# Turning normalised h of layers 0 and 1 by transposing DMA on 16-bit planes instead of by TensorE

## The chip, the cores and the metric

The kernel runs on one core of a Trainium2 chip. The metric is the device time of one execution in microseconds (us), and the time of a kernel is the median of its runs. Before the change it is 1192.94 us (three runs, 1192.58 to 1193.06).

## The reference, cut to what matters

Four graph layers work on x of shape (8, 2048, 64), float32, with one adjacency matrix adj of 2048 x 2048. Each layer normalises x, takes the positive part and adds what the layer makes of it:

```
h = max(layernorm(x), 0)                     # before every layer
# layer 0: w = einsum(embedding, weight), per node; b = embedding @ bias
x = x + sum_k einsum(A_k h, w[:, k]) + b     # A_0 = I, A_1 = adj, A_2 = 2 adj adj - I
# layer 1: v = h with node 0 replaced by intervention_value, then 3 times:
v = relu([v, adj v] @ W1.T + b1) @ W2.T + b2
x = x + v
# layer 2: x + ((adj h / sqrt2) mixed by w_nl, + b_nl) @ w_out.T + b_out
# layer 3: x + elu(softmax over neighbours with adj > 0.5, or over all nodes) applied to h
```

What matters here is that layers 0 and 1 need h in two positions. The products with adj want the nodes on the partitions. The term A_0 h of layer 0 and the first v of layer 1 want the features on the partitions, so that a small weight matrix can be applied to them. A block of h is therefore turned: 128 x 512 numbers with nodes on the partitions become 128 x 512 numbers with features on the partitions.

## The kernel before, in words

The 8 samples go in 4 pairs p (two samples of 64 features fill 128 columns), and the 2048 nodes in 4 blocks nb of 512. A block is a tile of 128 partitions x 4 x 128 float32, 256 KB. The matrix lies in SBUF as BT with entries 0 or 1. A product of h with it (`chunks`, L261) takes 16 chunks of 128 nodes, and in each two matmuls, one with the high part H of h and one with the rest L; the result is scaled by a row `crow` on VectorE (`scaled`, L246).

**Layer 0.** A prologue (up to about 84 us) loads the matrix, normalises the pairs 0 and 1, writes their h to the DRAM tensors hs and makes their first products. Then, for each p and nb (loop at L805 to L881), TensorE makes the second product t2T (32 matmuls) and then, in `node_weights` (L767), for each of four t twelve pairs of matmuls y (L781) of the turned terms t0T, t1T, t2T with the weights. VectorE multiplies each y by the node's embedding and adds it up (L790, 16 times for each t), and y has two buffers. After the block `keep` (L759) normalises the result for layer 1, and stores h in hs and x in xs. In pass p = 0 every block also normalises a block of pair 2 (`norm_0(2, nb)`, L881); pair 3 is normalised in the products of pass p = 2.

A normalisation (`norm_stages`, L180) runs in three stages that later calls of `go_on` release: means and squares (ScalarE, tile sq, which has one buffer), variances (VectorE) and a power (GpSimd, L200), and the scaling of z (VectorE, L203, tile z with three buffers), after which `done` or `store` is called.

**The turning.** `to_feat` (L278) turns a block: four TensorE transposes into PSUM (`transposed`, L271, L275) and one ScalarE copy (L280). It serves two users. `feat_0` (L800) loads h of the next block (queue of ScalarE, tile hb_f) and turns it into t0T, between the product t2T of a block and its y matmuls. `begin_next` (L727) loads h of a pair of layer 1 (tile hb), overwrites the first node with the intervention value (L740) and turns it into gT. For pair 0 of layer 1 this happens in the last block of layer 0: `between` calls `first_operand(t)` (L743) after each t, which turns block t and multiplies it by a weight (`back_whole`, L715, the tile bn_u). For the pairs 1 to 3, `step1` (L942) calls it at chunks 4 and 12 of the last product of the pair before (dictionary `fill`, L1022) and at chunk 4 of its own first product (L997); `halve_two` (L748) then makes the operand from two blocks.

**Layer 1** makes three steps for each pair, each with four products of 32 matmuls, and small ones (ph L953, bn L708) between them. In the steps 0 and 1 VectorE also tests whether the matrix is what this path assumes (`test`, L911): `test_load` (L900) loads a strip of adj and a transposed strip mt of a copy of BT, by a transposing DMA of 128 x 512 two-byte numbers on the queue of SyncE (L908).

What sets the order: the program order above, from which the framework's scheduler makes one fixed order of instructions for each engine and queue when the kernel is built; `issue_after`, which puts one instruction behind another on its engine; and the `fill` dictionaries. At run time each engine and each queue takes its instructions in that order and waits where an operand or a buffer isn't ready.

Of the kernel before, what the change touches and what calls it, by code (L numbers as in the profile page):

```python
# [8 lines left out]
F32 = mybir.dt.float32  # L9
F32R = mybir.dt.float32r  # L10
BF16 = mybir.dt.bfloat16
I32 = mybir.dt.int32
U8 = mybir.dt.uint8
AF = mybir.ActivationFunctionType
ALU = mybir.AluOpType
AX = mybir.AxisListType
# [26 lines left out]
def uniform_path(  # L43
# [53 lines left out]
    biasD = dram.tile([P, NCH, C], F32, name="biasD")  # L97
    t1D = dram.tile([P, N], F32, name="t1D")
    MD = dram.tile([N, N], BF16, name="MD")

    def bank(tag, name):
        return psums[-1].tile([P, 512], F32, tag=tag, name=name)
# [51 lines left out]
    def load_h(p, nb, name, pool):  # L154
        t = pool.tile([P, 4, 2 * C], F32, tag="hb", name=f"hb_{name}", bufs=2 if lastp else 3)
        (nc.sync if lastp else nc.scalar).dma_start(t, hs[p][:, part(nb), :])
        return t

    def load_crow(nb, name, tag="crow"):
        t = work.tile([P, 512], F32, tag=tag, name=f"crow_{name}", bufs=2)  # L160
# [132 lines left out]
    def norm_0(p, nb, also=None, xt=None):  # L293

        def done(z):
            if also is not None:
                also(z)
            stored.append(
                (nc.gpsimd if xt is None else nc.scalar).dma_start(hs[p][:, part(nb), :], z)
            )  # L300

        if xt is not None:
            return norm_stages(xt, f"0_{p}_{nb}", done, None)
        norm_relu(load_x(0, p, nb), f"0_{p}_{nb}", done)
# [338 lines left out]
    def make_weights():  # L643

        col(b1[:, None], 1, "b1c", b1c)
        b2c = col(b2[:, None], 1, "b2c")
        bnl = col(b_nl[:, None], 1, "bnl")
        wn = col(w_nl, 2, "wnl")
        ws = consts.tile([P, 1], F32, name="wsum")

        raw = block("z", "wz0", 3)
        nc.gpsimd.memset(raw, 0.0)
        for i, w in enumerate((w1[:, :C], w1[:, C:], w2, w_out)):
            for hf in range(2):
                hs_ = slice(hf * C, (hf + 1) * C)
                nc.sync.dma_start(raw[hs_, i, hs_], w)
        yield
        tr, pr = (block("z", f"wz{i}", 3) for i in (1, 2))
        nc.vector.tensor_copy(tr, transposed(lambda t: raw[:, t, :], "wT"))
        nc.vector.tensor_copy(w1e, tr[:, 1])  # L660
        ps = psums[-1].tile([P, 4, P], F32, tag="tr", name="wP")
        b2b, bnb = b2c.to_broadcast([P, P]), bnl.to_broadcast([P, P])
        pairs = ((raw[:, 2], tr[:, 0]), (raw[:, 2], tr[:, 1]), (b2b, tr[:, 1]), (bnb, tr[:, 3]))
        for i, (lhsT, rhs) in enumerate(pairs):
            nc.tensor.matmul(ps[:, i, :], lhsT, rhs, start=True, stop=True)
        nc.vector.tensor_copy(pr, ps)
        p1 = bank("tr", "wb1s")
        nc.tensor.matmul(p1[:, :1], tr[:, 0], b2c, start=True, stop=True)
        nc.vector.tensor_tensor(b1s, p1[:, :1], b1c, op=ALU.add)

        fill_row(raw[:, 0, :], b_out)
        nc.vector.tensor_tensor(pr[:, 3, :], pr[:, 3, :], raw[:, 0, :], op=ALU.add)
        with tc.issue_after(chain[-1].ins):
            nc.vector.tensor_scalar(wn, wn, INV_SQRT2, None, op0=ALU.mult)
            nc.vector.tensor_tensor(ws, wn[:, 0:1], wn[:, 1:2], op=ALU.add)
        nc.vector.tensor_scalar(tr[:, 3, :], tr[:, 3, :], ws, None, op0=ALU.mult)
        for hf in range(2):
            with tc.issue_after(wt_load.ins):
                nc.sync.dma_start(ivt[:, hf * C:(hf + 1) * C], iv)
        nc.gpsimd.dma_start(wD[:, 0:4], tr)  # L680
        nc.gpsimd.dma_start(wD[:, 4:8], pr)
        yield


    w1e = consts.tile([P, P], F32, name="w1e")
    ivt = consts.tile([1, P], F32, name="ivt")

    def feat(i, name):

# [37 lines left out]
    def begin_next(n, q):  # L727

        if n >= len(items):
            return  # L730
        layer, p = items[n]
        nm = f"{layer}_{p}_{q}"
        hl, gT = ops.setdefault(n, ([], []))
        h = load_h(p, q, nm, lastp[0] if n else l0q)
        if layer == 2:
            hl.append(halves(h, nm))
            return
        if q == 0:
            with tc.issue_after(relus[-1].ins) if relus else nullcontext():
                nc.scalar.copy(h[0:1, 0, :], ivt)  # L740
        gT.append(to_feat(h, feat(0, f"gT_{nm}"), nm))

    def first_operand(q):  # L743
        begin_next(0, q)
        hl, gT = ops[0]
        hl.append(halves(back_whole(gT[q], w1e, f"u_{q}"), f"u_{q}"))

# [8 lines left out]
    def rows4(r, times=4):  # L756
        return r.rearrange("p (b c) -> p b c", b=2)[:, None].to_broadcast([P, times, 2, C])

    def keep(p, nb, acc, name, more):  # L759

        norm_relu(acc, name, lambda z: nc.gpsimd.dma_start(hs[p][:, part(nb), :], z))
        nc.gpsimd.tensor_tensor(nodes(acc), nodes(acc), more, op=ALU.add)  # L762
        kept.append(nc.gpsimd.dma_start(xs[p][:, part(nb), :], acc))

# [2 lines left out]
    def node_weights(p, nb, terms, between):  # L767
        acc = load_x(0, p, nb)
        bn = l0q.tile([P, 4, C], F32, name="bn", bufs=2)
        nc.sync.dma_start(bn, biasD[:, part(nb), :])  # L770

        odd = l0q.tile([P, 4, 2 * C], F32, name="odd")
        av, ov = nodes(acc), nodes(odd)
        for t in range(4):
            ts = slice(t * P, (t + 1) * P)
            for dg in range(D // DG):
                y = psums[-1].tile([P, 2, 512], F32, tag="big", name=f"y_{p}_{nb}_{t}_{dg}")
                for k in range(K):
                    for bb in range(2):
                        hs_ = slice(bb * C, (bb + 1) * C)  # L780
                        nc.tensor.matmul(  # L781
                            y[:, bb, :], terms[k][hs_, ts], wt[hs_, k, dg * 512:(dg + 1) * 512],
                            start=(k == 0), stop=(k == K - 1),
                        )
                for d in range(DG):
                    e = dg * DG + d
                    yd, ec = y[:, :, d * C:(d + 1) * C], emb[:, 4 * nb + t, e:e + 1]
                    xj = (av, ov)[d % 2][:, t]
                    old = xj if e != 1 else bn[:, t, None, :].to_broadcast([P, 2, C])
                    last = nc.vector.scalar_tensor_tensor(  # L790
                        xj, yd, ec, old, op0=ALU.mult, op1=ALU.add
                    )
            ahead.append(last)
            chain.append(last)
            go_on()
            between(nb, t)
        nc.vector.tensor_tensor(acc, acc, odd, op=ALU.add)
        keep(p, nb, acc, f"1_{p}_{nb}", b2r[:, None, None].to_broadcast([P, 4, 2, C]))

    def feat_0(p, q):  # L800
        h = h_first if p + q == 0 else load_h(p, q, f"f0_{p}_{q}", l0q)
        return to_feat(h, term(0, f"t0T_{p}_{q}"), f"0_{p}_{q}")

    first_t0 = []
    for p in range(NP):  # L805
        hl_next, t1T_next = [], []

# [18 lines left out]

        def between(nb, t):

            if 4 * p + nb + 1 == 4 * NP:
                first_operand(t)  # L830
            elif nb == 2 and t == 1:
                halve_next(0)
            elif nb == 3:
                halve_next(t + 1)
                if t == 0:
                    load_next(3)
# [16 lines left out]
        for nb in range(NB):  # L853
# [1 line left out]
            crow = load_crow(nb, nm)  # L855
            t2T = product(
                hl1, nb, nm, term(2, f"t2T_{nm}"), crow,
                fill={12: lambda: first_t0.append(feat_0(0, 0))} if p + nb == 0 else {},
                tag="mm" if p + nb else "b6",
            )  # L860
            if p + nb == 0:
                t0T = first_t0[0]
            go_on()
            t0T_next = feat_0(*divmod(4 * p + nb + 1, 4)) if 4 * p + nb + 1 < 4 * NP else None
            if p + nb == 0:
                pro.close()
                psums.append(ctx.enter_context(
                    tc.tile_pool(name="psum", bufs=2, space=bass.MemoryType.PSUM)
                ))
            if nb == 3:  # L870
                load_next(2)
            node_weights(p, nb, (t0T, t1T[nb], t2T), between)
            t0T = t0T_next
            if nb in (1, 2):
                load_next(nb - 1)
            with tc.issue_after(kept[-1].ins):
# [65 lines left out]
    def step1(n, p, st, hl, gT):  # L942
# [51 lines left out]
        halves_of = range(NCH // 2), range(NCH // 2, NCH)  # L994
        ps0 = sums_of(0)
        other = n > 0 and st == 0
        chunks(ps0, hl, 0, halves_of[0], {4: lambda: begin_next(n, 3)} if other else {})  # L997
        if carry:
            carry.pop()()
        if other:  # L1000
# [10 lines left out]
        add(1)  # L1011
        go_on()
        ps2 = sums_of(2)
        chunks(ps2, hl, 2, range(NCH))
        scale(ps2, 2)
        map_two(2)
        finish_two(0)
        add(2)
        go_on()
        fill = {}  # L1020
        if last:
            fill = {  # L1022
                4: lambda: (begin_next(n + 1, 0), begin_next(n + 1, 1)),
                9: lambda: halve_two(n + 1, 0), 12: lambda: begin_next(n + 1, 2),
            }
        ps3 = sums_of(3)
        chunks(ps3, hl, 3, range(NCH), fill)
# [740 lines left out]
```

## Time and profile before

| | |
|---|---|
| median of the runs | 1192.94 us |
| profiled execution, its own time | 1195.87 us |
| span of its profile | 1194.1 us |
| TensorE matmul (PE) busy | 1171.6 us, 98% |
| weight load (PEld) busy | 815.9 us, 68% |
| VectorE (DVE) busy | 744.7 us, 62% |
| ScalarE (ACT) busy | 235.5 us, 20% |
| GpSimd (POOL) busy | 230.8 us, 19% |
| transposes of L275 that turn h (hb_f, hb, h_first) | 60, 64 and 4 |
| transposing DMAs (mt, L908) | 64 |
| granted TensorE clock | 0.997 |

The profile comes from one execution, so its span is compared with its own time of 1195.87 us, 2.93 us above the median of the runs. In a group line the columns are line, engine, operation, output and inputs by the program's names, shapes and count. In a line of the timeline they are start in us, duration in us, engine, line, operation, and in brackets how long the engine was idle before it and what released it. Matmuls are pipelined: the distance between two starts is what one costs, and the duration shown is longer. "SPq", "ACTq" and "POOL ... DMA" are transfers being issued by a queue.

### The profile page before, as it was taken

What the parts mean: (1) busy time and instruction counts of PE and PEld (TensorE: products, weight loads), DVE (VectorE), ACT (ScalarE), POOL (GpSimd) and SP (SyncE); (2) the same over time, 40 slices, a digit from 0 to 9 for tenths busy, and PEclk for the clock granted to TensorE, in tenths of its full rate; (3) what the DMA queues carried; (4) which work ended last, traced back from release to release, by engine and by line L of the source; (5) the groups of instructions that cost most, each with busy time, mean ns of one, the idle gap of its engine ahead of it and who ended that gap; (6) DMA issues with size and microseconds to landing.
All of it is one profiled execution on the core that took longest, in us unless ns stands there. A gap on an engine that the chain in (4) does not pass through costs nothing.

```text
span 1194.1 us, 19514 instructions
## 1 busy us (share of the span) xinstructions
PE 1171.6 (98%) x7738; PEld 815.9 (68%) x7738; DVE 744.7 (62%) x1933; ACT 235.5 (20%) x372; POOL 230.8 (19%) x244
## 2 busy tenths in 40 slices
PE   8999999999999999999999999999999999999995
PEld 7775555555585555855547777777778777778884
DVE  5457888877847777267764446554644655465674
ACT  5620001000010000000012224333322433211110
POOL 5520221211121111001102004101300410241121
PEclk9999999999999999999999999999999999999998
DMA  9982334222241233212217634662763374351432
GB/s 359 330 209 66 93 102 119 84 67 79 81 141 45 75 82 100 78 31 73 69 55 195 132 80 129 173 142 72 193 132 83 125 177 103 106 170 60 136 114 74
DMA packets 99848, 141.24 MB, mean 118 GB/s; under 512 B 43772, under 2 KB 56572, under 8 KB 97700
## 3 DMA queue, kind: packets, MB, share of 16 engines
q1 hardware_dynamic: 81332, 79.43, 25.6%
q0 software_dynamic: 12256, 49.73, 13.9%
q10 hardware_dynamic: 6160, 10.75, 2.9%
q8 instruction: 63, 1.03, 0.3%
q14 instruction: 37, 0.30, 0.1%
HBM read 95.03 MB, written 35.66 MB: 109 GB/s over the span
## 4 chain that ended last, share of the span: by engine, by line
PE 90%; DVE 3%; DMA 3%; ACT 1%; POOL 1%; issue 1%; POOLq 0%; DVEq 0%; ACTq 0%
PE bv L264 38%; PE y L781 27%; DMA BT<-in_adj_dram 3%; PE bv_3b L264 3%; PE bv_2b L264 3%; PE bv_1b L264 3%; PE bv_0b L264 2%; PE bn L708 2%; PE ph L953 2%; PE pt L275 1%; PE bv_0a L264 1%; PE bv_3a L264 1%; PE bv_2a L264 1%; PE bv_1a L264 1%; DVE acc L790 1%
## 5 line engine op out<-in xcount | busy, mean ns | idle before, releaser
L264 PE MATMUL bv<-BT,H 128*128 128x512 f32 x768 | 303.4, 395 | 0.0
L264 PE MATMUL bv<-BT,L 128*128 128x512 f32 x768 | 299.3, 390 | 0.0
L790 DVE SCALAR_TENSOR_TENSOR acc<-y,emb,acc 128x128 f32<-128x128 f32 x512 | 176.2, 344 | 66.0 <-PE y L781 66.0
L264 PEld LDWEIGHTS bv<-BT,H 128*128 128x128 f32 x768 | 144.1, 188 | 37.1 <-PE bn L708 6.5
L264 PEld LDWEIGHTS bv<-BT,L 128*128 128x128 f32 x768 | 144.2, 188 | 29.0
L790 DVE SCALAR_TENSOR_TENSOR odd<-y,emb,odd 128x128 f32<-128x128 f32 x448 | 153.3, 342 | 0.0
L781 PE MATMUL y<-wt,t0T 64*128 64x512 f32 x512 | 143.7, 607 | 2.4 <-DVE odd L790 1.7
L200 POOL TENSOR_TENSOR rstd<-var,mhalf 128x8 f32<-128x8 f32 x64 | 106.5, 1665 | 169.5 <-DVE var L197 165.2
L192 ACT ACTIVATE sq<-z 128x512 f32<-128x512 f32 x64 | 40.4, 632 | 410.9 <-DVE z L187 382.7
L264 PE MATMUL bv<-BT,H_u 128*128 128x512 f32 x256 | 100.9, 394 | 0.0
L249 DVE TENSOR_TENSOR g<-bv,crow 128x512 f32<-128x512 f32 x48 | 33.2, 691 | 108.4 <-PE bv L264 107.9
L264 PE MATMUL bv<-BT,L_u 128*128 128x512 f32 x256 | 99.8, 390 | 0.0
L781 PEld LDWEIGHTS y<-wt,t0T 64*128 64x128 f32 x512 | 45.8, 185 | 63.2 <-issue 57.1
L762 POOL TENSOR_TENSOR acc<-acc,b2r 128x512 f32<-128x512 f32 x16 | 21.2, 1325 | 314.5 <-DVE z L187 314.5
L762 POOL TENSOR_TENSOR acc<-acc,wl 128x512 f32<-128x512 f32 x16 | 22.1, 1381 | 306.0 <-DVE z L187 305.4
L203 DVE SCALAR_TENSOR_TENSOR z<-z,rstd 128x512 f32<-128x512 f32 x64 | 43.6, 686 | 39.1 <-POOL rstd L200 39.1
L781 PE MATMUL y<-wt,t1T 64*128 64x512 f32 x256 | 66.8, 589 | 0.0
L264 PEld LDWEIGHTS bv<-BT,H_u 128*128 128x128 f32 x256 | 48.1, 188 | 13.2 <-issue 3.2
L187 DVE SCALAR_TENSOR_TENSOR z<-mean,acc 128x256 f32<-128x256 f32 x112 | 52.7, 514 | 5.2 <-DMA hs<-z 4.7
L264 PEld LDWEIGHTS bv<-BT,L_u 128*128 128x128 f32 x256 | 48.1, 188 | 9.7
L959 ACT COPY g<-ph 64x512 f32<-64x512 f32 x64 | 37.2, 582 | 77.8 <-PE ph L953 76.6
L916 DVE SCALAR_TENSOR_TENSOR junk<-mt,cols,st 128x512 uint8<-128x512 bf16 x64 | 47.9, 748 | 5.2 <-DMA mt<-MD 3.8
(228 smaller groups left out, 1743.4 us busy)
## 6 DMA issues: line engine op xcount, KB each, us to landing
BT<-in_adj_dram POOLq DMA_DIRECT2D x16, 1024.0 KB, 10.8
crow<-crowD SPq DMA_DIRECT2D x64, 256.0 KB, 3.5
st<-in_adj_dram SPq DMA_DIRECT2D x64, 256.0 KB, 4.0
hs<-z POOLq DMA_DIRECT2D x40, 256.0 KB, 3.2
xs<-acc POOLq DMA_DIRECT2D x32, 256.0 KB, 2.8
MD<-BT POOLq DMA_DIRECT2D x16, 512.0 KB, 5.3
acc<-xs SPq DMA_DIRECT2D x32, 256.0 KB, 4.6
hb<-hs SPq DMA_DIRECT2D x28, 256.0 KB, 3.3
```

The costliest lines, as they stand in the source:

```text
L187: firsts.append(nc.vector.scalar_tensor_tensor(split(z)[:, :, e], each(mean)[:, :, e, None].to_broadcast([P, 4, C]), -1.0 / C, nodes(xt)[: ...
L192: squares.append(nc.scalar.activation(sq, z, AF.Square))
L200: powers.append(nc.gpsimd.tensor_tensor(rstd, var, mhalf, op=ALU.pow))
L203: scales.append(nc.vector.scalar_tensor_tensor(groups(h), g, 0.0, rstd[:, :, None].to_broadcast([P, 8, C]), op0=ALU.max, op1=ALU.mult))
L249: ahead.append(nc.vector.tensor_tensor(to, ps.rearrange("p (q t) -> p t q", t=4), crow, op=ALU.mult))
L264: nc.tensor.matmul(ps, hl[m // 4][i][:, m % 4, :], BT[:, m, nb * 512:(nb + 1) * 512], start=(m == 0 and i == 0), stop=(m == NCH - 1 and i ...
L708: nc.tensor.matmul(ps[two[hf], bb, (4 * i + t) * C:(4 * i + t + 1) * C], fT[two[bb], at:at + C], wmat[two[bb], two[bb]], start=True, stop= ...
L762: nc.gpsimd.tensor_tensor(nodes(acc), nodes(acc), more, op=ALU.add)
L781: nc.tensor.matmul(y[:, bb, :], terms[k][hs_, ts], wt[hs_, k, dg * 512:(dg + 1) * 512], start=(k == 0), stop=(k == K - 1),)
L790: last = nc.vector.scalar_tensor_tensor(xj, yd, ec, old, op0=ALU.mult, op1=ALU.add)
L916: nc.vector.scalar_tensor_tensor(junk, mt, cols[:, i, :], st, op0=ALU.mult, op1=ALU.not_equal, accum_out=bad[:, i, q:q + 1],)
L959: nc.scalar.copy(gT[nb + i][two[bb], :], ph[bb][two[bb ^ i], :])
```

## The change

Turned h of both layers, but for the very first block, no longer comes from TensorE. Each block of normalised h is seen as 16-bit numbers and split on ScalarE into two planes, the low and the high halves (`store_planes`, two copies that read every second 16-bit number; they land in the tile sq). GpSimd's queue writes both planes to a DRAM tensor hp. SyncE's queue brings each plane back with a transposing DMA into a tile hb (`load_planes`, two DMAs), and ScalarE joins them (`join_planes`, two copies that write every second 16-bit number).

Blocks of layer 0 that the prologue has normalised are in hs only, so pass p = 0 loads seven of them again and splits them (`restage`, two in each block). The pairs 2 and 3 are split where they are normalised, and `keep` of layer 0 splits instead of storing h in hs. The calls of `begin_next` move: for pair 0 into the blocks 2 and 3 of the last pass, for the others partly from the last product of a pair to the one before it; `first_operand(3)` moves from the last block of layer 0 to chunk 7 of layer 1's first product. The intervention value becomes a column that is copied into gT after the join.

```diff
+    hp = [[
+        dram.tile([NB, 2, P, 512], U16, name=f"hp{layer}_{p}") for p in range(NP)
+    ] for layer in range(2)]
...
+    def bits(t):
+        return t.bitcast(U16)
+
+    def store_planes(h, layer, p, nb):
+
+        pl = bits(block("sq", f"pl_{layer}_{p}_{nb}", 1).rearrange("p t f -> p (t f)"))
+        hv = bits(h.rearrange("p t f -> p (t f)")).rearrange("p (q s) -> p s q", s=2)
+        pl = pl.rearrange("p (s q) -> p s q", s=2)
+        for s in range(2):
+            nc.scalar.copy(pl[:, s], hv[:, s])
+        nc.gpsimd.dma_start(hp[layer][p][nb].rearrange("s p q -> p s q"), pl)
+
+    def load_planes(layer, p, nb, pool):
+        t = pool.tile([P, 512], F32, tag="hb", name=f"pt_{layer}_{p}_{nb}", bufs=2 if lastp else 3)
+        pt = bits(t).rearrange("f (s n) -> f s n", s=2)
+        for s in range(2):
+            nc.sync.dma_start(
+                pt[:, s],
+                hp[layer][p][nb, s].rearrange("p (t f) -> (p t) f", t=4),
+                transpose=True,
+            )
+        return pt
+
+    def join_planes(pt, out):
+        ov = bits(out).rearrange("f (t n s) -> f s t n", t=4, s=2)
+        for s in range(2):
+            nc.scalar.copy(ov[:, s], pt[:, s].rearrange("f (n t) -> f t n", t=4))
+        return out
...
             stored.append(
                 (nc.gpsimd if xt is None else nc.scalar).dma_start(hs[p][:, part(nb), :], z)
             )
+            if xt is None:
+                store_planes(z, 0, p, nb)
...
-        for hf in range(2):
-            with tc.issue_after(wt_load.ins):
-                nc.sync.dma_start(ivt[:, hf * C:(hf + 1) * C], iv)
+        col(iv.rearrange("o c -> c o"), 1, "ivt", ivt)
...
-        h = load_h(p, q, nm, lastp[0] if n else l0q)
         if layer == 2:
-            hl.append(halves(h, nm))
+            hl.append(halves(load_h(p, q, nm, lastp[0]), nm))
             return
+        pt = load_planes(1, p, q, lastp[0] if n else l0q)
+        with tc.issue_after(relus[-1].ins) if relus else nullcontext():
+            gT.append(join_planes(pt, feat(0, f"gT_{nm}")))
         if q == 0:
-            with tc.issue_after(relus[-1].ins) if relus else nullcontext():
-                nc.scalar.copy(h[0:1, 0, :], ivt)
-        gT.append(to_feat(h, feat(0, f"gT_{nm}"), nm))
+            nc.scalar.copy(gT[0][:, 0:1], ivt)
 
     def first_operand(q):
-        begin_next(0, q)
...
+             lambda z, p, nb: store_planes(z, 1, p, nb))
...
+    def restage(times):
+
+        for _ in range(times):
+            p, q = divmod(len(restaged) + 1, NB)
+            if p > 1:
+                return
+            h = block("z", f"h_{p}_{q}", 3)
+            restaged.append(nc.sync.dma_start(h, hs[p][:, part(q), :]))
+            store_planes(h, 0, p, q)
...
+            if t == 2 and ahead_t0:
+                join_planes(*ahead_t0)
+            if p + 1 == NP and t == 3 and nb > 1:
+                begin_next(0, 3 * (nb - 2))
             if 4 * p + nb + 1 == 4 * NP:
-                first_operand(t)
+                if t == 0:
+                    begin_next(0, 2)
+                if t < 3:
+                    first_operand(t)
...
-            t0T_next = feat_0(*divmod(4 * p + nb + 1, 4)) if 4 * p + nb + 1 < 4 * NP else None
...
+            if p == 0:
+                restage(2)
             if nb == 3:
                 load_next(2)
+            if 4 * p + nb + 1 < 4 * NP:
+                at = divmod(4 * p + nb + 1, NB)
+                ahead_t0 = [load_planes(0, *at, l0q), term(0, "t0T_%d_%d" % at)]
+            if 4 * p + nb + 1 == 4 * NP:
+                begin_next(0, 1)
             node_weights(p, nb, (t0T, t1T[nb], t2T), between)
...
-        chunks(ps0, hl, 0, halves_of[0], {4: lambda: begin_next(n, 3)} if other else {})
+        fill = {}
+        if st == 0:
+            fill = {4: lambda: begin_next(n, 3)} if n else {7: lambda: first_operand(3)}
+        chunks(ps0, hl, 0, halves_of[0], fill)
...
-        chunks(ps2, hl, 2, range(NCH))
+        fill = {}
+        if last and n + 1 < NP:
+            fill = {5: lambda: begin_next(n + 1, 0), 11: lambda: begin_next(n + 1, 1)}
+        chunks(ps2, hl, 2, range(NCH), fill)
...
-        if last:
+        if last and n + 1 < NP:
+            fill = {6: lambda: begin_next(n + 1, 2), 9: lambda: halve_two(n + 1, 0)}
+        elif last:
             fill = {
                 4: lambda: (begin_next(n + 1, 0), begin_next(n + 1, 1)),
-                9: lambda: halve_two(n + 1, 0), 12: lambda: begin_next(n + 1, 2),
+                12: lambda: begin_next(n + 1, 2),
             }
```

More of the change, by code (lines that the diff above doesn't have):

```diff
@@ L13 @@
 U8 = mybir.dt.uint8
+U16 = mybir.dt.uint16
 AF = mybir.ActivationFunctionType
@@ L685, in uniform_path @@
     w1e = consts.tile([P, P], F32, name="w1e")
-    ivt = consts.tile([1, P], F32, name="ivt")
+    ivt = consts.tile([P, 1], F32, name="ivt")
     def feat(i, name):
@@ L757, in rows4, with store_h, keep @@
         return r.rearrange("p (b c) -> p b c", b=2)[:, None].to_broadcast([P, times, 2, C])
-    def keep(p, nb, acc, name, more):
-        norm_relu(acc, name, lambda z: nc.gpsimd.dma_start(hs[p][:, part(nb), :], z))
+    def store_h(z, p, nb):
+        nc.gpsimd.dma_start(hs[p][:, part(nb), :], z)
+    def keep(p, nb, acc, name, more, store=store_h):
+        norm_relu(acc, name, lambda z: store(z, p, nb))
         nc.gpsimd.tensor_tensor(nodes(acc), nodes(acc), more, op=ALU.add)
@@ L797, in node_weights @@
         nc.vector.tensor_tensor(acc, acc, odd, op=ALU.add)
[L798 to L804, printed above, removed]
+        keep(p, nb, acc, f"1_{p}_{nb}", b2r[:, None, None].to_broadcast([P, 4, 2, C]),
+             lambda z, p, nb: store_planes(z, 1, p, nb))
+    first_t0, restaged = [], []
+    def restage(times):
[6 more added lines that the diff above has]
+            store_planes(h, 0, p, q)
     for p in range(NP):
@@ L857, in uniform_path @@
                 hl1, nb, nm, term(2, f"t2T_{nm}"), crow,
-                fill={12: lambda: first_t0.append(feat_0(0, 0))} if p + nb == 0 else {},
+                fill={12: lambda: first_t0.append(
+                    to_feat(h_first, term(0, "t0T_0_0"), "0_0_0")
+                )} if p + nb == 0 else {},
                 tag="mm" if p + nb else "b6",
@@ L863, in uniform_path @@
             go_on()
-            t0T_next = feat_0(*divmod(4 * p + nb + 1, 4)) if 4 * p + nb + 1 < 4 * NP else None
+            ahead_t0 = []
             if p + nb == 0:
@@ L869, in uniform_path @@
                 ))
+            if p == 0:
+                restage(2)
             if nb == 3:
                 load_next(2)
+            if 4 * p + nb + 1 < 4 * NP:
[3 more added lines that the diff above has]
+                begin_next(0, 1)
             node_weights(p, nb, (t0T, t1T[nb], t2T), between)
-            t0T = t0T_next
+            t0T = ahead_t0[-1] if ahead_t0 else None
             if nb in (1, 2):
```

## The prediction, made before the result was known

> **What bounds the kernel now.** I read the busy times first, then the chain of work that ended last, then the timeline of TensorE around the transposes, and last the groups of the tiles that the change touches.
>
> ```profile
> PE 1171.6 (98%) x7738; PEld 815.9 (68%) x7738; DVE 744.7 (62%) x1933; ACT 235.5 (20%) x372; POOL 230.8 (19%) x244
> PE 90%; DVE 3%; DMA 3%; ACT 1%; POOL 1%; issue 1%; POOLq 0%; DVEq 0%; ACTq 0%
> L275 PE MATMUL pt<-ident,hb x64: 270/273/331, 600.1 to 941.0; 128*128 128x128 f32 x64
> L275 PE MATMUL pt<-ident,hb_f x60: 270/272/300, 91.1 to 566.0; 128*128 128x128 f32 x60
> ```
>
> A busy TensorE proves little, since its durations overlap; but 90% of the chain is TensorE too. So TensorE's instruction stream sets the end, and what leaves it is time gained unless another wait ends last there. The change takes out both groups, 124 transposes (31 blocks). Their 272 ns isn't the price, since they overlap. The timeline of TensorE gives it, at a change from product to y matmuls with a transposed block, at the one such change without (last block of layer 0), and in layer 1:
>
> ```profile
> 120.58 0.39 PE L264 MATMUL bv_1b<-BT,L_t 128*128 128x512 f32 x1
> 120.81 0.60 PE L275 MATMUL pt<-ident,hb_f 128*128 128x128 f32 x4
> 121.34 1.13 PE L781 MATMUL y<-wt,t0T 64*128 64x512 f32 x4
> ...
> 594.42 0.39 PE L264 MATMUL bv_3b<-BT,L_t 128*128 128x512 f32 x1
> 594.74 1.13 PE L781 MATMUL y<-wt,t0T 64*128 64x512 f32 x4
> ...
> 720.68 0.39 PE L264 MATMUL bv<-BT,L 128*128 128x512 f32 x1
> 721.27 1.09 PE L275 MATMUL pt<-ident,hb 128*128 128x128 f32 x8 [0.20 <-ACT hb L740]
> 722.12 0.47 PE L264 MATMUL bv<-BT,H 128*128 128x512 f32 x1
> 722.43 0.39 PE L264 MATMUL bv<-BT,L 128*128 128x512 f32 x1
> ```
>
> With the block 0.76 us pass between the last product matmul and the first y, without it 0.32. A layer 0 block costs 0.44 us.
>
> But VectorE is close behind in some blocks. The timelines of TensorE and ScalarE in the second block of pass 0:
>
> ```profile
> 132.38 1.13 PE L781 MATMUL y<-wt,t0T 64*128 64x512 f32 x4 [0.42 <-DVE odd L790]
> ...
> 122.33 0.63 ACT L192 ACTIVATE sq<-z 128x512 f32<-128x512 f32 x1 [0.24 <-DVE var L195]
> 148.00 0.63 ACT L192 ACTIVATE sq<-z 128x512 f32<-128x512 f32 x1 [25.04 <-DVE z L187]
> ```
>
> At 132.38 TensorE waited for VectorE to empty a y buffer. The waits of TensorE list four such, 1.7 us in all; the chain has VectorE in it at 132, 222, 309 and 457. ScalarE is idle for 25 us there.
>
> [...] This trace has 64 of that size (128 KB) and type, so I use their durations:
>
> ```profile
> L908 SPq DMA_TRANSPOSE mt<-MD x64: 1121/1122/2070, 632.0 to 1002.0; - x64
> DMA to landing us min/median/max: 3.3/4.1/7.0
> ```
>
> [...] 586 for the copy L280 (out of PSUM), 601 to 626 for the cast of hb. No row shows 16-bit numbers at a stride. [...] casts on ScalarE that wait up to 22.2 us for one operand. So an early copy that isn't ready holds all behind it.
>
> **The change, part by part.**
>
> *Layer 0, transposes out.* 15 blocks. The first, turned just before the y matmuls of block (0,0), is followed by a wait: y starts at 92.38, 0.68 us after being ready, because of ScalarE's copy L280 of the next block. From the last product matmul at 90.56 to 92.38 are 1.82 us, where 0.32 would do. But a change of PSUM pool lies there, which can wait for the scaling that ends at 91.69. Gain between 0.6 and 1.5; I take 0.8. The other 14 have 0.44 each. Where VectorE already holds TensorE up (four of the 14), an earlier y only lengthens that wait: 0. In the two others of pass 0, with the same VectorE load, I count half. 8 x 0.44 + 2 x 0.22 = 4.0.
>
> *Pair 0 of layer 1.* After y at 599.56 the next would have come at 599.99; a transpose (600.09), two y matmuls, a wait for gT (bn_u at 601.73) and bn_u follow, and y goes on at 602.82. That is 2.8 us, of which 0.43 are y. With gT joined beforehand, bn_u's 1.09 and some 0.2 for the two changes of tile shape remain: a gain of 1.1 for each of three, 3.3. The fourth now waits from 624.37 to 625.63 for its transpose and copy, 1.26. Moved to chunk 7 it doesn't; but wl, issued at 624.40 after the last y and 512 KB long, is needed there 4.9 us after the last y instead of 6.1, and a 512 KB store (MD) takes 5.3 us. And the PSUM buffer of bn_u must be emptied (0.6 + 0.7 us and two hand-overs) before the second product may start, with only 1.02 us of ph in between. 1.26 less some 1.2: 0.
>
> *Pairs 1 to 3.* From 720.91 (0.23 after the last product matmul) to 722.12 plus a first matmul 0.08 longer: 1.29 for the two blocks, including 0.36 of waiting for the intervention copy L740. The next block (727.20 to 727.55, and 0.09 after it) costs 0.44, the last the same. 2.17 x 3 = 6.5.
>
> *ScalarE.* Four copies for each of 31 blocks for one: 124 x 0.6 - 31 x 0.586 = +56 us, so about 292, 24% busy. In layer 0 it has the idle 25 us. In layer 1 a join (two copies, 1.25) stands where a copy of 0.59 was. The tightest is block 3 of a pair: its slot in t1 comes free when the previous pair's last sum is made, and it follows that relu, which ends 2.65 us after the last product matmul (731.88 against 729.23). 1.25 later is 3.9; halve_two needs it after eight chunks (3.67) and bn (1.09), 4.76. Cover 0.8 us; if the copies cost twice as much, TensorE waits about 0.5 in each of three. At half price nothing is gained, as they are off the path. I take 0.
>
> *SyncE's queue.* 62 transposes x 1.12 = 70 us and 7 reloads x 0.32. They stand ahead of loads of acc, bn and crow, but that queue only waits for some 20 us in each block (92 to 111.6, for a bn buffer). Even behind that bn load the planes would land near 111.9 + 2.2 + 4.1 = 118, and y of the next block starts at 121.3: 0. ScalarE's queue loses 15 loads (5 us, off the path).
>
> *GpSimd's queue.* 31 stores for 16 stores of h: 15 x 0.6 = 9 us of 81% idle time. The power L200 behind them can be late where a store waits for ScalarE; that is in the next item.
>
> *The new wait.* The planes use tile sq, one buffer. It is free again only when the store has landed: 1.25 for the copies, 3.2 landing (median of hs<-z from GpSimd), between 0.3 and 0.9 of hand-overs: 4.8 to 5.4 us. In blocks 1 and 2 of pass 0 there are four such (two restaged, one for layer 1, one for pair 2) between the last variance (ends 123.7) and the next squares at 148.0. 4 x 4.8 to 5.4 = 19 to 22 of 24.3 us. So they fit, narrowly: from 6.1 us a cycle the squares are late, then VectorE's variance, and behind it in its queue the y sums, and TensorE waits. The reload of h (tile z, 4 us) and casts H_t queued behind a waiting copy on ScalarE can add to it. Bounds: 0 and about 20; I take 1.5.
>
> Sum: 0.8 + 4.0 + 3.3 + 0 + 6.5 - 1.5 = 13.1. Against the profiled execution's 1195.87 that is 1182.8 (span 1181.0); against the median 1192.94 it is 1180.
>
> **The rivals.**
> *A, the forecast:* TensorE's transposes are gone and little else moves: 1175 to 1186. Chance 0.55.
> *B, the gain is mostly eaten in layer 0:* VectorE sets the pace wherever it is close, and joins or squares come late a little in each block of pass 0. The 4.8 of layer 0 go and 3 more are lost: 1192.9 - 9.8 + 3 = 1186, up to 1190.5. For it: the four waits on L790. Against: VectorE is 62% busy, and passes 1 to 3 carry one normalisation less a block. Chance 0.13.
> *C, slower: the single sq buffer.* Reloads, stores and GpSimd's power delay one another in pass 0, so that a cycle takes 8 us (stores of t1D took up to 7.6). Then 4 x 8 - 24.3 = 8 us late in each of two blocks, which TensorE waits out: 16 us, and 1180 + 16 = 1196. It decides from 6.1 us a cycle, and eats the whole gain at some 7.7. For it: DMA's share is 33 to 40% in these blocks, 20 to 26% in passes 1 and 3. Against: the median landing of 3.2 to 3.6. Slower 0.15, within 0.2% 0.07.
> *D, everything gains:* all 14 at 0.44, block (0,0) 1.5, the fourth bn_u 1.3, no loss: 6.2 + 1.5 + 4.6 + 6.5 = 18.8, so 1174. Chance 0.10.
> That the transposes stay on TensorE can't be, but for h_first's 4.
>
> **How the numbers follow.** Faster by over 0.2% (A, B, D): 0.78; within 0.2%, 2.4 us, about what a measurement of this kernel can tell from no change: 0.07; slower: 0.15. The likeliest is A, 1180. For 8 in 10 the range takes A and B, nearly all of D and the faster half of no change: 1172 to 1193.
>
> **What would show it.** The groups pt<-ident,hb and hb_f gone; ScalarE near 290 us; the distance from product to y at 0.32; bn_u in the last block of layer 0 followed by y 1.2 to 1.3 later; no wait of TensorE for joins at the start of a pair. A wait of VectorE's var for sq, or a first sq after 149 in pass 0, speaks for C; more waits of y on L790 for B. The prediction is wrong if TensorE's waits grow by more than some 5 us, or if the copies of 16-bit numbers take over 1.2 us.

## The result, and the profile after

The kernel after takes 1190.57 us (median of 20 runs, 1188.16 to 1194.05). The kernel before, run beside it, takes 1194.2 (20 runs, 1192.49 to 1197.21). The ratio is 0.9969, with a 95% interval of 0.996 to 0.9977: 3.6 us faster, where the forecast had 13.1. That lies within the stated range of 1172 to 1193, but far from the likeliest 1180. The profiled execution of after has a time of its own of 1192.25 us and a span of 1190.5.

The page of after, its busy times and its chain of waits, against the lines of the same place before:

```profile
PE 1157.7 (97%) x7614; PEld 801.9 (67%) x7614; DVE 740.6 (62%) x1933; ACT 293.5 (25%) x465; POOL 243.6 (20%) x259
...
PE 69%; issue 11%; DVE 7%; DMA 7%; POOL 3%; ACT 1%; POOLq 0%; DVEq 0%; ACTq 0%; SPq 0%
```

The 124 transposes are gone (7738 instructions of TensorE became 7614) and it is busy 13.9 us less. But the chain, which had TensorE in 90% of the span, has it in 69%. The time went into waits, and the next question is which. The waits of TensorE and of VectorE (engine, operation that waited, what it waited for: us in total, times, longest), the lines of before under those of after:

```profile
PE y L816 <- DVE odd L825: 7.7, 6, 5.8
PE bv L297 <- DVE L_u L274: 3.7, 4, 2.3
...
PE y L781 <- DVE odd L790: 1.7, 4, 0.4
```

```profile
DVE L_t L274 <- ACT H_t L272: 17.5, 7, 6.6
...
DVE acc L1028 <- DMA acc<-xs: 11.7, 4, 4.3
...
DVE L_t L241 <- ACT H_t L239: 6.9, 5, 2.0
```

The y matmuls had waited at most 0.4 us at a time for these sums, and L_t at most 2.0 for H_t; the sum L1028 (L969 before) had waited 0.6 us once for its reload. So there are two new waits. The table sets the traces against each other; it counts from the first y matmul of block (0,0), since where that lies varies from execution to execution (89.7 to 94.8 us over the profiled runs of this study) with work ahead of it that the change hardly touches. The matmuls ph are those that layer 1 makes between its products, and pS are the last layer's sums over the nodes.

| us | before | after |
|---|---|---|
| first y of (0,0) to first y of (3,3) | 502.36 | 505.00 |
| of it block (0,2), first y to next block's first y | 29.61 | 37.17 |
| first y of (3,3) to last ph of layer 1 | 435.81 | 428.38 |
| first ph of pair 1, 2, 3 to its second | 19.33, 19.34, 19.33 | 22.15, 20.04, 20.58 |
| last ph to the last pS | 153.18 | 153.48 |

Layer 0 lost 2.6 us, and only because block (0,2) lost 7.6. Layer 1 gained 7.4, and would have gained 12.2 without the 4.8 that the starts of pairs 1 to 3 lost.

**Block (0,2).** The timeline of ScalarE in after, and then the line of the same cast in before:

```profile
152.49 1.14 ACT L172 COPY pl<-h 128x512 uint16<-128x512 uint16 x2 [0.75 <-DVE var L228]
159.10 1.14 ACT L172 COPY pl<-h 128x512 uint16<-128x512 uint16 x2 [5.47 <-DMA hp<-pl]
163.46 1.14 ACT L172 COPY pl<-z 128x512 uint16<-128x512 uint16 x2 [3.23 <-DMA hp<-pl]
167.54 1.14 ACT L172 COPY pl<-z 128x512 uint16<-128x512 uint16 x2 [2.94 <-DMA hp<-pl]
168.59 0.58 ACT L272 CAST H_t<-pt_t 128x512 fp32r<-128x512 f32 x1
...
162.09 0.59 ACT L239 CAST H_t<-pt_t 128x512 fp32r<-128x512 f32 x1 [9.63 <-DMA hs<-z]
```

Four pairs of plane copies, two of restaged blocks, one for layer 1 and one for pair 2, stand in ScalarE's order ahead of the cast H_t. Its operand has been ready since about 161 (TensorE makes pt_t from 160.27 on). Each pair of copies but the first waits until the store of the pair before it has landed. The next two fences follow that into VectorE and TensorE:

```profile
169.20 0.69 DVE L274 TENSOR_TENSOR L_t<-pt_t,H_t 128x512 fp32r<-128x512 f32 x1 [6.55 <-ACT H_t L272]
169.81 0.34 DVE L825 SCALAR_TENSOR_TENSOR acc<-y,emb,acc 128x128 f32<-128x128 f32 x1
```

```profile
165.25 1.02 PE L816 MATMUL y<-wt,t2T_2b 64*128 64x512 f32 x4
172.10 2.08 PE L816 MATMUL y<-wt,t0T 64*128 64x512 f32 x4 [5.83 <-DVE odd L825]
173.94 1.94 PE L816 MATMUL y<-wt,t1T 64*128 64x512 f32 x4
```

L_t holds VectorE's queue for 6.55 us. The y sums that empty TensorE's PSUM buffers stand behind it, and TensorE waits 5.83. Then four y matmuls take 1.84 us (172.10 to 173.94) instead of 0.86, as the granted clock is 0.50 there (last section); by 176.69 that has cost 2.0 more. 5.8 and 2.0 make up the loss: 7.6, and the 0.44 that the block should have gained.

**Starts of pairs.** The timeline of VectorE at the first pair change of layer 1 in after, with the same two sums in before as the last line, and that of GpSimd in after just ahead of it:

```profile
728.73 0.69 DVE L1028 TENSOR_TENSOR acc<-bn,acc 128x512 f32<-128x512 f32 x1 [1.16 <-PE bn L741]
733.69 0.69 DVE L1028 TENSOR_TENSOR acc<-bn,acc 128x512 f32<-128x512 f32 x1 [4.27 <-DMA acc<-xs]
...
736.15 0.69 DVE L274 TENSOR_TENSOR L_u<-bn_u,H_u 128x512 fp32r<-128x512 f32 x1
...
734.44 1.29 DVE L969 TENSOR_TENSOR acc<-bn,acc 128x512 f32<-128x512 f32 x2 [2.52 <-PE bn L708]
```

```profile
722.52 1.31 POOL L797 TENSOR_TENSOR acc<-acc,wl 128x512 f32<-128x512 f32 x1
723.77 1.67 POOL L233 TENSOR_TENSOR rstd<-var,mhalf 128x8 f32<-128x8 f32 x1
725.40 0.60 POOL L798 DMA_DIRECT2D xs<-acc  x1
```

There are two acc buffers. The second sum of a pair's last two needs a buffer that must first be stored to xs and then loaded anew. Before, the store left GpSimd directly after its addition (725.68 + 1.31, store at 727.29), and the two sums came from 7.15 us later on, held up by TensorE alone. Now a power stands between the addition and the store, the second sum's turn comes 4.0 us after the store, and it waits 4.27 us for the reload. The L_u of the second operand stands behind it, and TensorE waits 2.34 us at 736.89.

The same wait comes a fourth time where layer 2 begins, 2.45 us at 1046.13.

The last rows are those of the new operations (busy us, mean ns of one, idle before) and of the plane stores (KB, median us from issue to landing):

```profile
L172 ACT COPY pl<-z 128x512 uint16<-128x512 uint16 x48 | 27.3, 616 | 129.4 <-DVE z L236 99.6
...
L189 ACT COPY t0T<-pt 128x512 uint16<-128x512 uint16 x30 | 21.1, 763 | 135.5 <-PE y L816 132.6
...
hp<-pl POOLq DMA_DIRECT2D x31, 256.0 KB, 2.6
```

### The profile page after: what moved, and what is told of

The parts are those of the page before. It is cut to its first block, busy times and chain, and to the rows that moved or that the text cites. A ratio compares the mean times of both kernels' runs of the same rounds, so it can differ in the third digit from the quotient of the medians.

```text
span 1190.5 us, 19465 instructions
## 1 busy us (share of the span) xinstructions
PE 1157.7 (97%) x7614; PEld 801.9 (67%) x7614; DVE 740.6 (62%) x1933; ACT 293.5 (25%) x465; POOL 243.6 (20%) x259
## 4 chain that ended last, share of the span: by engine, by line
PE 69%; issue 11%; DVE 7%; DMA 7%; POOL 3%; ACT 1%; POOLq 0%; DVEq 0%; ACTq 0%; SPq 0%
PE bv L297 26%; PE y L816 25%; PE bv_1b L297 3%; PE bv_2b L297 3%; PE bv_3b L297 3%; DMA BT<-in_adj_dram 2%; POOL rstd L233 2%; PE bn L741 2%; DMA acc<-xs 1%; PE bv_0a L297 1%; PE bv_0b L297 1%; PE bv_2a L297 1%; PE ph L1012 1%; PE bv_1a L297 1%; DVE z L220 1%
## 5 line engine op out<-in xcount | busy, mean ns | idle before, releaser
L825 DVE SCALAR_TENSOR_TENSOR odd<-y,emb,odd 128x128 f32<-128x128 f32 x448 | 154.2, 344 | 0.0
L816 PE MATMUL y<-wt,t0T 64*128 64x512 f32 x512 | 138.9, 611 | 8.5 <-DVE odd L825 7.7
L172 ACT COPY pl<-z 128x512 uint16<-128x512 uint16 x48 | 27.3, 616 | 129.4 <-DVE z L236 99.6
L189 ACT COPY t0T<-pt 128x512 uint16<-128x512 uint16 x30 | 21.1, 763 | 135.5 <-PE y L816 132.6
```

What stands on the lines that cost most here:

```text
L172: nc.scalar.copy(pl[:, s], hv[:, s])
L189: nc.scalar.copy(ov[:, s], pt[:, s].rearrange("f (n t) -> f t n", t=4))
L816: nc.tensor.matmul(y[:, bb, :], terms[k][hs_, ts], wt[hs_, k, dg * 512:(dg + 1) * 512], start=(k == 0), stop=(k == K - 1),)
L825: last = nc.vector.scalar_tensor_tensor(xj, yd, ec, old, op0=ALU.mult, op1=ALU.add)
```

## The experiments

The theory: two queues in fixed order lose what TensorE gains. Its part A: in block (0,2) the cast H_t stands on ScalarE behind plane copies that wait for one buffer. Its part C: in layer 1 the sum L1028 waits for a reload of one of two acc buffers. Their rivals B and D are in the expectations; the letters of this section are not those of the prediction's rivals. All kernels compute everything. The kernel before took 1195.09 beside the first four (11 runs), 1194.84 beside the next four (43) and 1194.8 beside the last two (11). A ratio is to these runs of it; that of after is 0.9969 (0.996 to 0.9977).

**planes_own.** In pass 0 the planes use a slot of the L tiles instead of the one buffer sq.

```
-        pl = bits(block("sq", ...))
+        if p == 0 or layer == 0 and p < 3:
+            pl = bits(spare("L", f"pl_{layer}_{p}_{nb}"))
+        else:
+            pl = bits(block("sq", ...))
```

> In pass 0 of layer 0 the planes use a slot of the six of tag L instead of the one buffer sq; nothing else changes. Theory A (ScalarE's fixed order puts the cast H_t of block 2 behind four pairs of plane copies, and each pair waits until the planes before it have landed): the copies no longer wait for a landing, the cast comes back from 168.6 to about 162, TensorE's wait of 5.8 us on L825 goes, and the time falls from 1190.6 to about 1184 (1182 to 1186). Rival B (the extra transfers slow the loads of pass 0, the buffer is not the reason): the cast stays near 168 and the time at 1190.6.

Measured: 1185.33, ratio 0.9915 (0.9899 to 0.9931). That is 5 us better than after and within what A says. But the trace shows the cure at work only in part. In it the cast runs at 163.16, as early as before. Then:

```profile
166.29 0.69 DVE L277 TENSOR_TENSOR L_t<-pt_t,H_t 128x512 fp32r<-128x512 f32 x1 [4.83 <-DMA hp<-pl]
```

L_t now waits for a plane store itself, since it needs an L slot that planes hold; block (0,2) takes 35.2. This execution was the slowest of six (1191.07; the others 1182.8 to 1187.0). So the edit put a wait of its own in place of the one it removed. What its trace does show is that the cast comes early with all the transfers still in the block: it was the wait for the buffer that held it, not the transfers.

**restage_early.** The seven restaged blocks are reloaded four and three in blocks (0,0) and (0,1), none in (0,2).

```
-                restage(2)
+                restage((4, 3, 0, 0)[nb])
```

> The seven blocks of h that pass 0 reloads and splits are taken four in block 0 and three in block 1, instead of two, two, two and one; sq stays the one buffer. Theory A: block 2, the first with a cast H_t, has two pairs of plane copies ahead of it and not four, so the cast comes near 164 and the time falls to about 1185 (1183 to 1187); block 1 has five pairs and may lose up to 1 us. Rival B: as many transfers in less time, so 1190.6 or slower.

Measured: 1183.29, ratio 0.9907 (0.9887 to 0.9926). ScalarE's timeline in this kernel:

```profile
158.18 1.14 ACT L172 COPY pl<-z 128x512 uint16<-128x512 uint16 x2 [6.26 <-DVE z L236]
162.42 1.14 ACT L172 COPY pl<-z 128x512 uint16<-128x512 uint16 x2 [3.10 <-DVE odd L825]
163.46 0.58 ACT L272 CAST H_t<-pt_t 128x512 fp32r<-128x512 f32 x1
```

With two pairs ahead of the cast instead of four it runs at 163.46, and block (0,2) takes 29.96 instead of 37.17. No buffer was added and no copy taken away, and the block gets back 7.2 us. Together with planes_own, which kept the transfers in place, this shows A. Some 0.8 us are not got back, as 29.61 before less a gain of 0.44 would be 29.17.

**acc_three.** The third block of each pair in layer 1 loads its x into an accumulator of its own, so there are three. To make room, a small tile of the last layer (`four`) shares a buffer with another (`junk`).

```
-                    acc = load_x(1, p, nb + i)
+                    if nb + i == 2:
+                        acc = lastp[0].tile([P, 4, 2 * C], F32, tag="acc1", ..., bufs=1)
+                        fill_x(acc, 1, p, 2)
+                    else:
+                        acc = load_x(1, p, nb + i)
```

> In layer 1 block 2 of each pair takes x into a third buffer of its own, so that its load need not wait for the store of block 0. Theory C (with TensorE ahead by 2 us, VectorE's sum L1028 waits for the reload of an acc buffer that has first to be stored, and L_u queues behind it): the 4.3 us wait at the start of pair 1 shrinks, and of the 4.8 us lost at the start of the pairs 1 to 3 at least half comes back: 1186 to 1188.5. Rival D (the load stands behind the transposing DMAs in SyncE's queue, or the joins on ScalarE are late): 1190.6.

Measured: 1185.64, ratio 0.9919 (0.9904 to 0.9935), 5 us better than after and a little better than expected. In its trace no sum waits for a reload, and each of the three pairs needs 19.33 to 19.34 us from its first ph to its second, as before. Block (0,2) still takes 38.2. C is shown, and that it is apart from A.

**early_acc.** Both edits at once.

> Both edits: the reloads four and three, and the third buffer. Theories A and C: the gains add up, about 1181 (1178 to 1184). Rivals B and D: 1190.6; one of them alone right: 1185 to 1187.

Measured: 1178.07 (1177.45 to 1179.13), ratio 0.9856 (0.9838 to 0.9873). The two losses add up, and with both cured the kernel is 17 us faster than before. Not all of that need belong to the change: from the last ph to the last pS it takes 152.22 us, 1.0 less than before. All five kernels with a third accumulator have 152.20 to 152.22 there, those with two from 152.2 to 154.2. So a third accumulator may help the kernel before as well; that was not run. The chain of waits of this kernel has TensorE back at nearly what it was:

```profile
PE 88%; DVE 5%; DMA 2%; issue 2%; POOL 1%; ACT 1%; POOLq 0%; DVEq 0%; ACTq 0%
```

**layer0_only.** Layer 0 as after; in layer 1 TensorE turns h as before, so there is no plane copy for layer 1.

```
-             lambda z, p, nb: store_planes(z, 1, p, nb))
...
+        gT.append(to_feat(h, feat(0, f"gT_{nm}"), nm))
```

> Only layer 0's blocks are turned by DMA; layer 1 is as before, and keep stores h, not planes. Theory A: block 2 of pass 0 has three pairs of plane copies ahead of the cast H_t, not four, so it comes near 164.5 and costs about 3 us, and 0.9 in pass 2; the 15 blocks give 6.8. In all about 3 us faster than before, ratio 0.9975 (0.995 to 1.0). Rival B (the extra transfers slow pass 0 as such): the 8 us stay, and it is 2 us slower than before, ratio 1.002.

Measured: 1192.33 (22 runs), ratio 0.9978 (0.997 to 0.9985). Block (0,2) takes 31.24. In ScalarE's timeline three pairs stand ahead of the cast (150.49, 157.16, 161.51), which runs at 162.56: only the fourth pair, that of layer 1, made the large loss. The time is as A expected.

**layer1_only, layer1_acc.** Layer 0 as before and layer 1 as after, with two accumulators and with three.

```
-            if xt is None:
-                store_planes(z, 0, p, nb)
...
-            if p == 0:
-                restage(2)
...
```

> Only layer 1's blocks are turned by DMA; layer 0 is as before, apart from the planes that keep splits. Theory A: one pair of plane copies ahead of the cast in block 2, so no loss in layer 0. Pair 0 gives 5.8, the pairs 1 to 3 give 6.4 and lose most of 4.8 at their starts to the reload of acc (theory C). About 7.5 us faster than before, ratio 0.9937 (0.992 to 0.996). Rival D (joins or the queue of SyncE are late in layer 1 as such): the same size, so this run doesn't tell C and D apart; the next one does.

> As layer1_only, with the third acc buffer in layer 1. Theory C: another 4 to 6 us, ratio to before about 0.9895 (0.987 to 0.992). Rival D: as layer1_only, 0.9937.

Measured: 1185.74, ratio 0.9919 (0.99 to 0.9938), and 1185.03, ratio 0.9915 (0.9897 to 0.9934). Two accumulators did better than expected, three worse, and the medians don't tell them apart, although only the first trace has the wait (pairs 19.33, 21.25 and 20.75, against 19.34 each). They were run once more for that, as layer1_only2 and layer1_acc2.

> The same edit as layer1_only: layer 1 changed alone, two accumulators. Theory, two accumulators cost 4 to 5 us at the starts of pairs 1 to 3 in every execution: 1188 to 1190, some 4 to 5 above layer1_acc2 beside it. Rival, the loss depends on when a reload lands and is small in many executions of this version: its median is within 1.5 us of layer1_acc2, and its times spread more widely.

> The same edit as layer1_acc: layer 1 changed alone, three accumulators. Theory and rival both: 1184 to 1185.5 with a narrow spread; the theory has layer1_only2 at 4 to 5 us more, the rival within 1.5.

Measured: 1186.38 (1183.04 to 1190.27), ratio 0.9921 (0.9897 to 0.9945), and 1182.71 (1182.18 to 1187.45), ratio 0.9891 (0.9867 to 0.9916). The difference of 3.7 lies between the two expectations. Over both times the runs with two accumulators have a median of 1186.2 (12 runs, 1182.04 to 1190.72) and those with three of 1184.2 (10 runs, 1181.56 to 1187.45). They are 2.0 apart and overlap so widely that with layer 1 changed alone a loss by C isn't shown by these times; it is shown by acc_three against after, and early_acc against restage_early, whose intervals lie apart. The pairs of layer1_only2 take 19.62, 19.70 and 20.33: a loss of 1.6 in this execution, 3.3 in the other and 4.8 in after. So C's size isn't fixed from execution to execution.

**one_acc.** acc_three, and one restaged block in each block of passes 0 and 1 instead of two in pass 0.

```
-            if p == 0:
-                restage(2)
+            if p < 2:
+                restage(1)
```

> One block of h reloaded and split in each of the first seven blocks of passes 0 and 1, and the third acc buffer; sq stays the one buffer. Theory A: block 2 has three pairs of copies ahead of the cast, block 1 three instead of five; the cast comes near 164 as with the reloads four and three: 1178 (1176 to 1180), as early_acc. Rival: since each reload now has to pass through DRAM within the block before it is used, the join is late and TensorE waits: over 1181.

Measured: 1197.24 (22 runs), ratio 1.0026 (1.0017 to 1.0035), 19 us above what was expected of it. Blocks (0,2) and (0,3) take 39.5 and 39.9. ScalarE's timeline says why:

```profile
159.99 0.77 ACT L189 COPY t0T<-pt 128x512 uint16<-128x512 uint16 x1 [8.82 <-DMA pt<-hp]
...
166.44 1.14 ACT L172 COPY pl<-z 128x512 uint16<-128x512 uint16 x2 [2.93 <-DMA hp<-pl]
167.49 0.58 ACT L272 CAST H_t<-pt_t 128x512 fp32r<-128x512 f32 x1
```

A block reloaded so late is needed in the very next block. Its join, which waits for the copy, the store and the transposes of those planes, is put ahead of the other plane copies and of H_t, and holds the queue for 8.82 us. It is A again with another operation at its head: fewer copies, in a worse place in the order, cost more. The theory's figure of 1178 counted copies and not places; the rival put down beside it, a join that comes late, is what happened.

## Why the prediction was wrong

**Where it failed: the new wait, taken at 1.5 us.** It measured 8.0 in block (0,2). Another 0.9 around the start of pass 2, where after takes 89.50 us from (1,3) to (2,1) and early_acc 88.55, isn't in every execution, since acc_three has the same layer 0 and takes 88.57. The step had the mechanism (copies that wait for one buffer), its bounds (0 to 20) and even the casts H_t behind a waiting copy. It failed in whom it made wait: it asked from what cycle on the next squares would be late, found room for four cycles in 24.3 us, and priced only that. The squares were not late. A cast that waits in the same queue was due at 161 to 162, some 9 us after the first copy, and no room was worked out for it: its operand was there from about 161, and it ran at 168.59, after the fourth pair of copies. Nor was a long cycle needed: after a first one of 6.61 us, in which the store took 4.4 us to land, they took 4.36 and 4.08, below the 4.8 to 5.4 assumed. The prediction's rival C had the right buffer with the same wrong victim: its 8 us in each of two blocks became 8 in one, at about half the cycle that it called for. (Three figures of the prediction are off without bearing on this. C's 1196 starts from 1180, which holds the 1.5 already, so its own terms give 1194.3. The DMA share of pass 1, set at 20 to 26%, is 26 to 32% by the blocks. And the casts that wait 22.2 us are released by a product matmul, so they wait for a buffer and not for an operand.)

**Where the number fits, it is luck.** The measured 1190.57 is the upper end of rival B, 1186 to 1190.5, and B's loss of 3 us in layer 0 is close to the 2.6 of the trace. But B had VectorE's pace and late joins cost a little in each block of pass 0, and the traces have one cast in one block; and layer 1 gave 7.4 instead of B's 9.8. One sign of being wrong came true: TensorE's waits for the y sums and for L_u grew by 6.0 and 3.7 us, where 5 was the limit.

**What it did not have: the reload of acc in layer 1.** The steps "pairs 1 to 3" and "pair 0" put what is late next, when TensorE gets 2 us ahead there, at nothing without saying so. In the trace of before the reload had a cover of some 2.1 us at the second pair change: issued at 834.8 it landed 2.7 us later, and its sum ran at about 839.7. The gain of some 2.2 us for each pair uses that up. Two things come on top in after. At the first pair change the store leaves GpSimd 1.57 us after the addition, where it was 0.30, and from the store's issue to the reload's landing 8.2 us pass (725.40 to 733.6), where it was 5.6 in before (831.95 to 837.5). That costs 4.8 over the three pairs in the profiled execution. Only where layer 2 begins did before have no cover at all:

```profile
1050.34 0.69 DVE L969 TENSOR_TENSOR acc<-bn,acc 128x512 f32<-128x512 f32 x1 [0.59 <-DMA acc<-xs]
```

**Pairs 1 to 3: right.** 6.5 forecast; the changes of pair shorten by 2.29, 1.81 and 2.28, 6.4 in all.

**Pair 0: too small.** 3.3 forecast, 6.25 measured, less 0.43 for a product that waits for L_u. Each of the first three gained 1.64 rather than 1.1. From one bn_u to the next 8.08 us pass in before and 6.44 in after (602.48 to 608.92). The 24 y matmuls between them take 5.15 at their pace of 0.858 for four, so in after 1.29 is left, as forecast: bn_u's 1.09, and 0.2 for the two changes of tile shape (0.96 us from start to start beside bn_u). The cost before was 2.93 and not 2.40. The fourth, taken at 0, gained 1.3, what is left of the 6.25: the late wl and the PSUM buffer, argued against it, held up little.

**Layer 0: right in size, wrong in part.** From product to y 0.31 us pass (120.30 to 120.61), as forecast. All the transitions gave 0.44, those too where VectorE holds TensorE up: in early_acc these waits come to 2.1 us in five places, against 1.7 in four. The likely reason, not tested by itself, is that a block's sums start with its own y matmuls and so move along with them. 14 x 0.44 = 6.2 instead of 4.0; with the 0.8 that stays in block (0,2) early_acc has 5.6. Block (0,0) can't be told from the spread of where it starts; TensorE still waits 0.8 us for t0T there.

**The engines off the path: right.** ScalarE 293.5 us for 292. The split copies take 616 ns, where 600 was the author's estimate; the joins take 763. Why a block is turned as two planes isn't shown by any run, as none turns it whole. Nothing waits for a join at the start of a pair, and SyncE's queue held nobody up: the two loads of acc go out at 724.34 and 729.4, ahead of the transposes (730.27).

With both waits away the trace of early_acc gives the sum: 5.6 us in layer 0, 11.6 in layer 1, 1.0 in layer 2, together 18.2. The profiled executions themselves differ by 16.7 (1195.87 and 1179.13), as the time ahead of the first y and behind the last pS is some 1.5 us longer, and the medians by 17.0. The gains were there, and larger than the 14.6 forecast; after lost 13.7 of them (1073.20 us from first y to last pS in early_acc, 1086.86 in after), nearly all in two queues. What stays open is how much of it a run that isn't profiled loses: the median gain of after is 3.6, its trace from first y to last pS gains 4.5, and the time from the last pS to the end of the span varies by itself, from 10.4 to 13.2 us over the traces.

## What to carry to other kernels

When an operation with a wait is put into an engine's queue, list everything behind it in that queue with the time at which each is due, and price the first that comes late (here H_t, due at 161 and run at 168.59); room before the next use of the buffer is not enough. When the bounding engine gets faster, work out by how much each reload and each operand was early in the kernel before (here 2.1 us), as what has less cover than the gain is late next. In these runs the place of such work in the order counted more than its amount: moving the reloads ahead by a block gave 7 us (restage_early against after), spreading them out cost 12 (one_acc against acc_three).

## What was not expected of the hardware

One pause of TensorE cost more than itself: 5.83 us, and 2.0 more of slower matmuls. The table of stretches in after (stretch, its length, busy time of each engine, and then the granted clock, DMA's share and GB/s):

```profile
166.00:172.00 6.00, 0.27 (x2) 0.00 (x0) 2.80 (x10) 1.62 (x3) 0.72 (x1) 0.76 0.25 87
172.00:176.00 4.00, 3.90 (x10) 1.98 (x12) 2.02 (x8) 0.00 (x0) 0.00 (x0) 0.50 0.02 4
176.00:178.00 2.00, 2.00 (x12) 0.85 (x11) 1.10 (x5) 0.24 (x1) 0.00 (x0) 1.00 0.00 0
732.00:736.00 4.00, 2.55 (x12) 1.75 (x10) 2.31 (x5) 0.00 (x0) 0.00 (x0) 1.00 0.66 94
```

After 5.83 us without work the clock is 0.50 for some 4 us, and four y matmuls take 1.84 us at first instead of 0.86. After the 2.34 us at the start of a pair it stays at 1.00 (from 737 to 741 too, when TensorE works again). In planes_own TensorE waits 4.11 us up to 169.19, and the clock is 0.85 from 168 to 170, 0.50 from 170 to 172 and 0.80 from 172 to 174. How long a pause has to be for this isn't shown.

A plane store of 256 KB from GpSimd's queue lands in 2.6 us (median of 31; the slowest took 5.6). With it copies of 1.14 us come in a cycle of 4.1 to 4.4 (159.10, 163.46, 167.54). A copy of 16-bit numbers that reads at a stride of two costs 616 ns (L172), about as much as the cast of 32-bit numbers H<-hb before (601 to 626), while one that permutes and writes at that stride costs 763 (L189).
